# A perceiver kernel: the running maximum of the first attention in float32r, turned by products with the identity

## The chip, the cores and the metric

The kernel runs on one core of a Trainium2 chip. The metric is the device time of one execution in microseconds; for a set of runs the median is given. A core has five engines that run side by side, each strictly in the order of its own queue: TensorE (PE; its weight loads are shown apart as PEld), VectorE (DVE), ScalarE (ACT), GpSimd (POOL) and SyncE (SP), which in this kernel issues the transfers. Products are written to PSUM; all else lies in SBUF or in the chip's main memory.

## The reference

Eight batches of 64 tokens of width 512 (`x`) pass six residual blocks. The first is a cross attention with a context of 1601 rows for each batch: 32 query heads share 8 key and value heads of width 128. The kernel's part at issue is its softmax.

```
q = (query @ Wq + bq).reshape(B, L, NKV, G, HDIM)        # 8 key heads, 4 query heads each
k_, v_ = jnp.split(kv @ Wkv + bkv, 2, axis=-1)
scores = jnp.einsum('blkgd,bmkd->bkglm', q, k) * scale
attn = jax.nn.softmax(scores, axis=-1)
o = jnp.einsum('bkglm,bmkd->blkgd', attn, v).reshape(B, L, NHEAD * HDIM)
return o @ Wo + bo
```

Then follow a state-space block (a scan over the tokens), a linear layer with ternary weights, a second cross attention on the raw context, a causal self attention and a gated feed-forward block, each on the layer-normed result of the one before.

## The kernel before

**Units.** The first attention is worked through in 64 units, one for each batch and key head. A unit handles 256 query columns (4 heads of 64 tokens) against 13 tiles of 128 context rows (the last has 65). Most of its products are float32r products of split operands: a number is kept as a high part in float32r and the rest, and three products (high-high, high-low, low-high) replace one in float32. `x_v` (L338) makes the values, `x_k` (L367) the keys, `x_s` (L389) the scores, `x_av` (L472) the weighted sum, `x_o` (L482) the softmax's denominator and `x_wo` (L522) the output product for pairs of batches. Values, keys, scores and the output product rotate through four PSUM buffers with the tag `kv`.

**The maximum.** Scores lie with the context rows on the partitions. While `x_s` makes them, two tiles at a time, ScalarE copies them from PSUM to the tile `S` (L392) and VectorE keeps an elementwise running maximum in `mx`, 128x512 (L396; L394 for the last tile of 65 rows; L399 folds the two halves to 128x256). In the next unit, `x_max` turns the two 128x128 halves of `mx` over on TensorE into the PSUM tile `m_ps` (L407), so that VectorE can take the maximum along the free axis (L409, to the float32r column `mc`, negated). `x_spread` spreads that column over all partitions by two float32r products, the column broadcast as the stationary operand and the identity as the moving one (L416). `x_exp` adds the result to the scores on VectorE (L430), takes the exponential on ScalarE (L431) and sums on GpSimd. The subtracted value is the same for all rows of a query column and cancels in the quotient.

**Order.** The rest of the blocks run as "side" generators between the steps of the attention, for groups of two batches: `halves` and `prep` lay out split and ternary weights in memory, and `chain` runs blocks two to six for a group. `run` advances them by costs that are written in the file. The program so recorded goes through a scheduler that moves instructions by its own estimate of their times, within their dependences; side instructions are partly pinned to program order. When the attention's last unit is recorded, the pools of the attention are freed, and the fourth group's chain runs with larger pools beside what is left of the third group's. In that last stretch the third group takes weights into `w_r` (L768) and multiplies by L777 and L778; the fourth group's self attention is the lines L1183 to L1226 with its output product at L761, and its feed-forward block begins at L1271. L1284 ends a SiLU with the gate's product, L1294 transposes its result, and L1306 is the last addition.

Of the kernel before, what the change touches and what calls it, by code (L numbers as in the profile page):

```python
# [8 lines left out]
FP = mybir.dt.float32  # L9
FR = mybir.dt.float32r  # L10
AF = mybir.ActivationFunctionType
ALU = mybir.AluOpType
# [4 lines left out]
P = 128  # L17
# [33 lines left out]
def rows_of(t):  # L51
    return TAIL if t == 12 else P
# [26 lines left out]
class Kernel:  # L79
# [293 lines left out]
    def x_s(self, b, i, st):  # L373

        nc = self.nc
        q = self.q[(b, i)]
        S = self.S.setdefault((b, i), [])
        if st == 0:
            self.mf[(b, i)] = self.sb("mx", [P, 2, 256], pool=self.xp, bufs=1)
        mx = self.mf[(b, i)]  # L380
        for g in [(2 * st, 2 * st + 1)] + ([(12,)] if st == 5 else []):
            sp = self.px.tile([P, 2, 256], FP, name=self.nm("s_ps"), tag="kv", bufs=KVB)
            r = P
            for gi, t in enumerate(g):
                r = rows_of(t)
                blk, o = self.at(t)
                kt = self.kt[(b, i, blk)]
                for k, (a, m) in enumerate(((0, 0), (0, 1), (1, 0))):
                    nc.tensor.matmul(sp[:r, gi, :], lhsT=kt[:, a, o : o + r], rhs=q[:, m, :], start=k == 0, stop=k == 2)  # L389
            s = self.sb("S", [P, 2, 256], pool=self.xp, bufs=SB)  # L390
            n = len(g)
            nc.scalar.copy(s[:r, :n], sp[:r, :n])  # L392
            if n == 1:
                nc.vector.tensor_tensor(mx[:r, 0], sp[:r, 0], mx[:r, 0], ALU.max)  # L394
            elif len(S) > 0:
                nc.vector.tensor_tensor(mx, sp, S[0] if len(S) == 1 else mx, ALU.max)  # L396
            S.append(s)
        if st == 5:
            nc.vector.tensor_tensor(mx[:, 0], mx[:, 0], mx[:, 1], ALU.max)  # L399

    def x_max(self, b, i):

        nc = self.nc
        m = self.mf.pop((b, i))
        ps = self.px.tile([P, 2, 256], FP, name=self.nm("m_ps"), tag="m", bufs=MB)
        for h in range(2):
            nc.tensor.transpose(ps[:, 0, h * P : (h + 1) * P], m[:, 0, h * P : (h + 1) * P], self.ident)  # L407
        col = self.sb("mc", [P, 2], FR, pool=self.xp, bufs=2)
        nc.vector.tensor_reduce(col, ps[:, 0].rearrange("p (h k) -> p h k", k=P), AX.X, ALU.max, negate=True)  # L409
        self.mm[(b, i)] = (ps, col)  # L410
# [1107 lines left out]
```

## Time and profile before

| What | Value |
|---|---|
| Median of 3 runs | 2667.18 us (2663.71 to 2670.01) |
| The profiled execution | 2656.56 us, its span 2654.8 us |
| PE, PEld busy | 2513.8 us (95%), 2241.6 us (84%) |
| DVE, ACT, POOL busy | 1671.4 us (63%), 1366.8 us (51%), 1291.8 us (49%) |
| Granted TensorE clock | 0.984 of full speed |
| The transposes L407, the spreading L416 | 128 instructions each |
| The running maximum L396, L394, L399 | 320, 64 and 64 instructions; 218.6, 26.8 and 36.5 us on DVE |

The span is what the profiler saw from the first to the last instruction; the execution's time includes what lies around it. A line of a group names the source line, the engine, the operation, the tile written and the tiles read, then how many there were. In lists of instructions in order of time the first column is the start in the span, the second the length, and a bracket at the end tells how long the engine had been idle and what ended that. Products of TensorE overlap, so their lengths add up to more than the time that passes; the distance from one start to the next tells what an instruction costs.

### The profile page before, as it was taken

What the parts mean: (1) busy time and instruction counts of PE and PEld (TensorE: products, weight loads), DVE (VectorE), ACT (ScalarE), POOL (GpSimd) and SP (SyncE); (2) the same over time, 40 slices, a digit from 0 to 9 for tenths busy, and PEclk for the clock granted to TensorE, in tenths of its full rate; (3) what the DMA queues carried; (4) which work ended last, traced back from release to release, by engine and by line L of the source; (5) the groups of instructions that cost most, each with busy time, mean ns of one, the idle gap of its engine ahead of it and who ended that gap; (6) DMA issues with size and microseconds to landing.
All of it is one profiled execution on the core that took longest, in us unless ns stands there. A gap on an engine that the chain in (4) does not pass through costs nothing. (4 is left out here: it accounts for less than half of the span.)

```text
span 2654.8 us, 43902 instructions
## 1 busy us (share of the span) xinstructions
PE 2513.8 (95%) x16192; PEld 2241.6 (84%) x16192; DVE 1671.4 (63%) x2747; ACT 1366.8 (51%) x3205; POOL 1291.8 (49%) x1305
## 2 busy tenths in 40 slices
PE   7999999999999999999999989999999999876888
PEld 6999899989989999987989888997898988864545
DVE  4545457665687766544567777554557687668755
ACT  4555554444556555544455555544456555445534
POOL 2445563463378655421356667632138467605420
PEclk9999999999999999999999999999999999987899
DMA  9799776675213244765425533654533543367676
GB/s 300 231 311 301 249 262 202 209 240 168 78 50 108 83 130 138 221 196 152 151 61 163 172 114 97 235 166 146 166 121 107 159 152 122 122 216 240 201 253 227
DMA packets 307672, 466.08 MB, mean 176 GB/s; under 512 B 91129, under 2 KB 187385, under 8 KB 302977
## 3 DMA queue, kind: packets, MB, share of 16 engines
q1 hardware_dynamic: 307456, 463.28, 54.2%
q8 instruction: 127, 2.08, 0.3%
q14 instruction: 89, 0.72, 0.1%
HBM read 389.66 MB, written 73.53 MB: 174 GB/s over the span
## 5 line engine op out<-in xcount | busy, mean ns | idle before, releaser
L367 PE MATMUL k_ps<-cxb,wk 128*128 128x384 f32 x2304 | 463.2, 343 | 28.3 <-ACT cxb L105 10.3
L338 PE MATMUL v_ps<-wv,cxb 128*128 128x256 f32 x3456 | 463.9, 282 | 1.3 <-DVE kt L109 1.2
L338 PEld LDWEIGHTS v_ps<-wv,cxb 128*128 128x128 f32 x3456 | 436.6, 189 | 16.7 <-issue 9.1
L367 PEld LDWEIGHTS k_ps<-cxb,wk 128*128 128x128 f32 x2304 | 399.2, 190 | 48.1 <-ACT cxb L105 10.7
L389 PE MATMUL s_ps<-q,kt 128*128 128x256 f32 (+1 forms) x2496 | 410.9, 298 | 9.6 <-DVE mx L396 4.2
L472 PE MATMUL o_ps<-S,v 128*128 128x256 f32 (+1 forms) x1664 | 409.9, 379 | 0.7 <-ACT v L341 0.4
L389 PEld LDWEIGHTS s_ps<-q,kt 128*128 128x128 f32 (+1 forms) x2496 | 338.9, 185 | 31.2 <-DVE mx L396 5.2
L460 POOL TENSOR_TENSOR ss<-ss,S 128x512 f32<-128x512 f32 x254 | 351.4, 1383 | 13.9 <-ACT S L431 0.9
L392 ACT COPY S<-s_ps 128x512 f32<-128x512 f32 (+1 forms) x448 | 241.8, 553 | 219.7 <-PE s_ps L389 216.2
L396 DVE TENSOR_TENSOR mx<-s_ps,mx 128x512 f32<-128x512 f32 x256 | 175.1, 684 | 285.0 <-ACT S L392 284.3
L472 PEld LDWEIGHTS o_ps<-S,v 128*128 128x128 f32 (+1 forms) x1664 | 298.7, 189 | 34.1 <-issue 1.4
L433 POOL TENSOR_TENSOR ss<-S,S 128x512 f32<-128x512 f32 x64 | 83.7, 1308 | 424.7 <-ACT S L431 377.0
L430 DVE TENSOR_TENSOR S<-S,m_ps 128x512 f32<-128x512 f32 (+1 forms) x448 | 257.8, 640 | 19.6 <-PE m_ps L416 19.4
L431 ACT ACTIVATE S<-S 128x512 f32<-128x512 f32 (+1 forms) x448 | 247.0, 600 | 44.3 <-DVE S L430 44.1
L108 ACT ACTIVATE kt<-k_ps,c_bk 128x384 fp32r<-128x384 f32 (+1 forms) x256 | 151.8, 593 | 211.9 <-PE k_ps L367 211.3
L109 DVE SCALAR_TENSOR_TENSOR kt<-k_ps,c_bk,kt 128x384 fp32r<-128x384 f32 (+1 forms) x256 | 160.7, 628 | 132.3 <-ACT kt L108 131.7
L341 ACT COPY v<-v_ps 128x256 f32<-128x256 f32 (+1 forms) x416 | 151.7, 368 | 162.2 <-PE v_ps L338 157.9
L338 PE MATMUL v_ps<-wv,cxt 128*128 128x256 f32 (+1 forms) x1536 | 208.6, 285 | 3.4 <-DVE kt L109 2.5
L338 PEld LDWEIGHTS v_ps<-wv,cxt 128*128 128x128 f32 (+1 forms) x1536 | 194.2, 177 | 12.9 <-DVE kt L109 3.8
L65 DVE TENSOR_TENSOR_SCAN a<-a,a 128x512 f32<-128x512 f32 x96 | 153.8, 1603 | 66.2 <-POOL a L65 66.0
L367 PE MATMUL k_ps<-cxt,wk 128*128 128x450 f32 x768 | 177.6, 374 | 0.3 <-ACT v L341 0.3
L65 ACT ACTIVATE a<-lv,c_A_log 128x128 f32<-128x128 f32 x384 | 123.2, 393 | 101.6 <-DVE a L65 100.8
(382 smaller groups left out, 3969.9 us busy)
## 6 DMA issues: line engine op xcount, KB each, us to landing
wo<-d_wo SPq DMA_DIRECT2D x127, 512.0 KB, 5.5
wk<-d_wk SPq DMA_DIRECT2D x63, 512.0 KB, 3.8
wv<-d_wv SPq DMA_DIRECT2D x31, 1024.0 KB, 5.8
cst<-in_ctxT_dram SPq DMA_DIRECT2D x96, 192.0 KB, 2.9
d_q<-q_t SPq DMA_DIRECT2D x32, 512.0 KB, 5.1
q<-d_q SPq DMA_DIRECT2D x64, 256.0 KB, 2.8
d_wo<-wo SPq DMA_DIRECT2D x32, 512.0 KB, 5.0
w<-d_wat SPq DMA_DIRECT2D x64, 256.0 KB, 3.3
```

The costliest lines, as they stand in the source:

```text
L65: return lambda *a, **k: self.tc.keep_in_program_order(f(*a, **k))
L108: nc.scalar.activation(hi, src, AF.Identity, bias=bias)
L109: eng.scalar_tensor_tensor(lo, src, bias, hi.bitcast(FP), ALU.add, ALU.subtract)
L338: nc.tensor.matmul(ps[:r], lhsT=cx[:, a, c, o : o + r], rhs=w[:, m, c, :], start=k == 0, stop=k == 11)
L367: nc.tensor.matmul(ps[:, :wd], lhsT=w[:, a, c, :], rhs=cx[:, m, c, :], start=k == 0, stop=k == 11)
L389: nc.tensor.matmul(sp[:r, gi, :], lhsT=kt[:, a, o : o + r], rhs=q[:, m, :], start=k == 0, stop=k == 2)
L392: nc.scalar.copy(s[:r, :n], sp[:r, :n])
L396: nc.vector.tensor_tensor(mx, sp, S[0] if len(S) == 1 else mx, ALU.max)
L430: nc.vector.tensor_tensor(sv, sv, ps[:r, 1:2].to_broadcast([r, w, 256]), ALU.add)
L431: nc.scalar.activation(sv, sv, AF.Exp, scale=ISC)
L460: nc.gpsimd.tensor_tensor(ss, ss, S[n], ALU.add)
L472: nc.tensor.matmul(ps[:, 0], lhsT=self.v[(b, j, t)][:r, hc : hc + P], rhs=S[t // 2][:r, t % 2], start=t == 0, stop=t == NT - 1)
```

## The change

The tile `mx` is declared float32r in place of float32. Every maximum writes it as float32r and reads it back through a float32 view, `mf`. The two transposes of `x_max` become two ordinary products: the half of `mx` is the stationary operand and the float32r identity the moving one. Their number, the tiles and the sizes stay.

```diff
         if st == 0:
-            self.mf[(b, i)] = self.sb("mx", [P, 2, 256], pool=self.xp, bufs=1)
+            self.mf[(b, i)] = self.sb("mx", [P, 2, 256], FR, pool=self.xp, bufs=1)
         mx = self.mf[(b, i)]
+        mf = mx.bitcast(FP)
...
             if n == 1:
-                nc.vector.tensor_tensor(mx[:r, 0], sp[:r, 0], mx[:r, 0], ALU.max)
+                nc.vector.tensor_tensor(mx[:r, 0], sp[:r, 0], mf[:r, 0], ALU.max)
             elif len(S) > 0:
-                nc.vector.tensor_tensor(mx, sp, S[0] if len(S) == 1 else mx, ALU.max)
+                nc.vector.tensor_tensor(mx, sp, S[0] if len(S) == 1 else mf, ALU.max)
             S.append(s)
         if st == 5:
-            nc.vector.tensor_tensor(mx[:, 0], mx[:, 0], mx[:, 1], ALU.max)
+            nc.vector.tensor_tensor(mx[:, 0], mf[:, 0], mf[:, 1], ALU.max)
...
         for h in range(2):
-            nc.tensor.transpose(ps[:, 0, h * P : (h + 1) * P], m[:, 0, h * P : (h + 1) * P], self.ident)
+            nc.tensor.matmul(ps[:, 0, h * P : (h + 1) * P], lhsT=m[:, 0, h * P : (h + 1) * P], rhs=self.ident_r, start=True, stop=True)
```

## The prediction

> **What bounds the kernel now.** I read the page's totals first, then the slices, then the table of stretches.
>
> ```profile
> span 2654.8 us, 43902 instructions
> PE 2513.8 (95%) x16192; PEld 2241.6 (84%) x16192; DVE 1671.4 (63%) x2747; ACT 1366.8 (51%) x3205; POOL 1291.8 (49%) x1305
> PE   7999999999999999999999989999999999876888
> ```
> ```profile
> 100.00:700.00 600.00, 590.62 (x3846) 556.07 (x3844) 346.70 (x606) 306.08 (x643) 297.59 (x278) 1.00 0.72 235
> 1300.00:1900.00 600.00, 582.42 (x3819) 521.69 (x3818) 380.99 (x599) 310.93 (x748) 311.63 (x316) 0.99 0.46 145
> 2330.00:2655.00 325.00, 252.16 (x1449) 166.76 (x1447) 214.24 (x418) 151.85 (x407) 94.94 (x100) 0.91 0.69 232
> ```
>
> In the stretches the columns after the length are the busy time of PE, PEld, DVE, ACT and POOL. Up to 2330 us TensorE is all but full: what it must issue sets the time, and every nanosecond of its issue counts. In the last 325 us it is busy for 252, so some 73 us are waits; there the order of its queue decides, since its products start in that order.
>
> The lines that the change touches are these, in the view of the tile `m_ps` (minimum, median, maximum in ns):
>
> ```profile
> L407 PEld LDWEIGHTS m_ps<-ident,mx x128: 137/140/144, 82.3 to 2332.9; 128*128 128x128 f32 x128
> L407 PE MATMUL m_ps<-ident,mx x128: 270/272/329, 82.4 to 2333.0; 128*128 128x128 f32 x128
> L416 PEld LDWEIGHTS m_ps<-ident,mc x128: 185/188/330, 86.0 to 2336.3; 128*128 128x128 f32 x128
> L416 PE MATMUL m_ps<-ident,mc x128: 219/273/415, 86.1 to 2336.4; 128*128 128x128 f32 x128
> ```
>
> L416 is the row to price by: it is already a pair of float32r products of a 128x128 operand with the identity, into the same PSUM tile. Durations overlap, so the cost is read from starts, in the timeline of PE:
>
> ```profile
> 82.43 0.38 PE L407 MATMUL m_ps<-ident,mx 128*128 128x128 f32 x2
> 82.56 0.96 PE L389 MATMUL s_ps<-q,kt 128*128 128x256 f32 x6
> ...
> 86.15 0.34 PE L416 MATMUL m_ps<-ident,mc 128*128 128x128 f32 x2
> 86.32 0.92 PE L338 MATMUL v_ps<-wv,cxb 128*128 128x256 f32 x6
> ```
>
> The work after a pair of transposes starts 0.13 us after the pair, the work after a float32r pair 0.17 us after it. Over all pairs the medians are 139 ns (61 pairs) and 170 ns (62 pairs), counted from when the pair could start to the next start. Inside, the two differ: the second transpose starts 108 ns after the first and the next product 28 ns later; the second float32r product starts 60 ns after the first and the next 110 ns later, because the weight load of the following product is what is late (loads start 108 ns apart).
>
> **The change, part by part.**
>
> *TensorE.* 64 heads times one pair: 64 x (170 - 139) ns = **+2.0 us**, all of it on the bound engine. Bounds: if the products ran 60 ns apart with nothing late behind, 120 ns a pair, -1.2 us; if each kept the 111 ns of the steady 128-column products of L962, 222 ns, +5.3 us. I take 170, from the same form.
>
> [...]
>
> *VectorE.* 448 instructions now write float32r (320 of L396, 64 each of L394 and L399). The rows of one operation in both types, PSUM and SBUF in, 512 wide: 681 ns to float32 (x19) and 683 ns to float32r (x11). 448 x 2 ns = 0.9 us on an engine at 63%: **0**. TensorE's long work beside it hides it; uncovered it would cost those 0.9 us.
>
> *Latency.* From the first start to the end of the second transpose it is 108 + 271 = 379 ns, of a float32r pair 60 + 273 = 333 ns: the reduction L409 may start 46 ns sooner. TensorE waits for it (L416 on L409) 5 times, 4.1 us in all up to 2330 us: at most 5 x 46 ns = 0.2 us, taken as 0. Nothing new is queued behind a wait: instructions, tiles and dependences are the same in number on all five engines.
>
> *Order.* The scheduler, which places instructions by its own estimates, builds another order. In the two built programs the first 575 of 14,400 TensorE instructions stand alike; 3785 stand elsewhere, 228 by over 30 places, 2291 of them in the last quarter. On SP 285 of 1307 moved (231 in the last quarter, 17 places at most), on POOL 259 of 1310 (at most 13). Up to 2330 us I take **0** for this: moved products are neighbours whose inputs mostly are ready, and TensorE's waits there are only 47 us, of many causes.
>
> In the last stretch two groups of batches run side by side: the third's products are L777/L778 on `w_r`, the fourth's the runs L1217, L1224, L761 and then L1271. Timeline of PE, before:
>
> ```profile
> 2606.58 0.43 PE L1224 MATMUL acc<-b,b 128*32 128x64 f32 x16
> ...
> 2613.43 0.60 PE L1294 MATMUL acc<-ident,b 128*128 128x128 f32 x4
> ...
> 2632.23 0.60 PE L1294 MATMUL acc<-ident,b 128*128 128x128 f32 x4
> 2634.49 0.50 PE L777 MATMUL acc<-w_r,b_r 128*128 128x512 f32 x1 [1.66 <-ACT b_r L105]
> ```
> ```profile
> 2622.10 10.02 PEld L1271 LDWEIGHTS acc<-s,b 128*128 128x128 f32 x48
> 2622.34 10.06 PE L1271 MATMUL acc<-s,b 128*128 128x512 f32 x48
> ```
> ```profile
> 2627.75 0.69 DVE L1284 TENSOR_TENSOR b<-b,b 128x512 f32<-128x512 f32 x1
> ```
>
> The fourth group's L1271 ran from 2622.34, and the third's second L1294 (with 16 products after it) only behind them. After the change these stand ahead of L1271, and so L1271 must wait for the third group's SiLU, which L1284 ended at 2628.44. The third group's first L1294 (2613.43 before) also moves forward, ahead of three rounds of L1224 that ran from 2606.58, which is 6.85 us earlier if its inputs allow. I take 6 of these: L1284 ends at 2622.4, plus transposes 0.6, copy and split 0.8, eight 512-wide products at 0.23 and eight 336-wide at 0.155 (3.1), makes L1271 start at about 2627.0: **+4.7 us**. If the third group is no earlier (its weights `w_r<-d_gu` came late then, 0.29 us of wait at 2605.24 with a transfer just landed), it is 2628.44 + 4.5 = 2632.9, about +10; if it is early enough, 0, or a gain of 3.4 us from work that no longer lies at the end.
>
> At the end of the attention the change gains: the last head's L416 ran at 2336.31, behind products that waited for a weight transfer, and now stands behind one float32 product of 0.8 us, at about 2333.9, 2.4 us sooner. It reaches the end only if the fourth group is what is late; with L1271 waiting for the third, it is swallowed. Taken as **0**, bound -2.4.
>
> Sum: 2.0 + 4.7 = **+6.7 us**. The profiled execution took 2656.56 us (span 2654.8 plus 1.8 around it), which would become 2663.3. It lies 10.6 us under the median of the three runs, 2667.18; on that scale the change gives **2674 us**. About 0.2% (5.3 us) is what a measurement can tell from no change; the three runs themselves spread over 6.3 us.
>
> **The rivals.**
>
> *Only the products' price counts* (same). The moves cancel: +2.0, or -0.4 with the earlier end of attention; 2667 to 2669. For it: nothing in dependences or work changes, and TensorE is 98% busy before 2330 us. Against it: the last stretch is all waits, and its order is much changed.
>
> *The waits for attention's PSUM buffers shrink* (faster). These rows are TensorE waiting until VectorE or ScalarE has emptied one of the four `kv` buffers:
>
> ```profile
> PE k_ps L367 <- DVE mx L396: 7.7, 6, 2.3
> PE s_ps L389 <- DVE mx L396: 4.2, 4, 1.9
> PE k_ps L367 <- DVE kt L109: 3.8, 3, 1.6
> PE v_ps L338 <- DVE kt L109: 3.7, 5, 1.1
> ```
>
> With L389 on L109, L367 on L394 and the small ones they make 26.8 us, and products of `o_ps`, which need no such buffer, change places with those that do. A third going is 8.9: 2.0 - 8.9 = -6.9, 2660 us. It decides once over 7.3 us (5.3 + 2.0) of the 26.8 go. Against it: waits can as well be made as lost.
>
> *The product is dearer than L416* (slower): 222 ns a pair, +5.3 us, 2672.5 with no loss by order. For it: L416's weights are one broadcast column, here they are a full matrix. Against it: both loads last 188 ns.
>
> That the change does nothing is excluded: another instruction form is issued.
>
> **How the numbers follow.** Forecast 0.38, dearer product 0.08, only the price 0.30, shrunken waits 0.24: slower 0.46, same 0.30, faster 0.24. The forecast's own range runs from L1271 at +0 (2.0) to L1271 at +10 with the product at its dearest (15.3): 2669 to 2682. For 8 in 10 the half spread of the three runs, 3.2, is added at the far ends: -6.9 - 3.2 gives 2657, 15.3 + 3.2 gives 2685.
>
> **What would show it.** Right: the pair of the new line to the next start near 0.17 us; its weight loads at 188 ns; L396 at 684 ns; TensorE's busy time up by some 2 us; L1271 starting behind a wait for the third group's products, 5 us later counted from the end of attention. Wrong: L1271 without a wait ahead of it and the last stretch shorter; the waits on `mx` and `kt` clearly away from 26.8 us; or a pair at over 0.2 us.

## The result: 0.8% slower, and the profile after

The changed kernel takes 2682.97 us (median; 2681.13 to 2685.43), the kernel before, on the same chip, 2665.44 us (2661.32 to 2670.01). The ratio is 1.0080, 95% interval 1.0063 to 1.0098: some 17 to 26 us slower. Slower was forecast, but as 2674 us. Lines behind L381 have moved on by one: L408 is the old L407, L1272 the old L1271.

The page's totals, and TensorE's slices:

```profile
span 2683.6 us, 43899 instructions
PE 2528.5 (94%) x16192; PEld 2253.8 (84%) x16192; DVE 1679.7 (63%) x2747; ACT 1364.1 (51%) x3205; POOL 1287.0 (48%) x1305
PE   7999999999999999999999989999999998966887
```

The span is 28.8 us longer than that of the profiled execution before (2656.56 us, quicker than the four above, while the one here is the slowest of its four, so the medians differ by less), and TensorE is busy for 14.7 us more. Up to 2330 us it is busy for 2261.6 and 2261.7 us: the difference comes to light at the end. The table of stretches of the changed kernel, for what comes behind 2330 us (the column behind GpSimd's is the granted clock, as a share of full speed):

```profile
2330.00:2690.00 360.00, 266.83 (x1471) 181.44 (x1470) 219.96 (x423) 155.21 (x417) 93.89 (x101) 0.86 0.63 211
```

The same stretch before had 252.16 us of TensorE (1449 records) at a granted clock of 0.91; here it is 266.83 us at 0.86. Part of that "busy" time goes with waiting: in e13 below, products of 512 columns behind a wait of 6.07 us run at a granted clock of 0.50 and last 0.63 us in place of 0.39. In the traces of the two kernels TensorE waits for over 4 us ten times behind the first 10 us (four times before, six in the changed kernel), and the granted clock of the 2 us behind each of these waits is 0.50.

The edited instructions, by the tile `m_ps` (durations as minimum/median/maximum in ns), and from the page's groups:

```profile
L408 PEld LDWEIGHTS m_ps<-ident,mx x128: 186/188/333, 80.1 to 2333.0; 128*128 128x128 f32 x128
L408 PE MATMUL m_ps<-ident,mx x128: 219/273/474, 80.2 to 2333.1; 128*128 128x128 f32 x128
L417 PE MATMUL m_ps<-ident,mc x128: 219/273/454, 83.9 to 2335.2; 128*128 128x128 f32 x128
```
```profile
L397 DVE TENSOR_TENSOR mx<-s_ps,mx 128x512 fp32r<-128x512 f32 x256 | 175.2, 684 | 286.7 <-ACT S L393 286.0
```

L408 has become L417's twin, as priced: counted from start to next start, the new pair takes 171 ns (median of 60 pairs; forecast 170), and the last one starts at 2333 us in both kernels. What the edit does directly is as forecast, and it is not the loss. The waits of TensorE show new rows:

```profile
PE acc L1295 <- DVE b L1285: 9.1, 2, 5.4
PE acc L778 <- ACT a L65: 6.1, 1, 6.1
PE acc L1218 <- POOL b L1210: 4.7, 1, 4.7
```

The first is the wait that was forecast: L1272 stands behind the third group's transposes L1295, and these wait for its SiLU, L1285. The timeline of PE there:

```profile
2644.70 1.09 PE L1295 MATMUL acc<-ident,b 128*128 128x128 f32 x4 [5.44 <-DVE b L1285]
2645.58 1.06 PE L731 MATMUL acc<-ident,b 128*128 128x128 f32 x4
...
2651.00 10.09 PE L1272 MATMUL acc<-s,b 128*128 128x512 f32 x48
```

L1272 starts 28.7 us later than before, and the end comes 28.8 us later.

### The profile page after: what moved, and what is told of

The parts are those of the page before. It is cut to its first block, busy times and chain, and to the rows that moved or that the text cites. A ratio compares the mean times of both kernels' runs of the same rounds, so it can differ in the third digit from the quotient of the medians.

```text
span 2683.6 us, 43899 instructions
## 1 busy us (share of the span) xinstructions
PE 2528.5 (94%) x16192; PEld 2253.8 (84%) x16192; DVE 1679.7 (63%) x2747; ACT 1364.1 (51%) x3205; POOL 1287.0 (48%) x1305
## 4 chain that ended last, share of the span: by engine, by line
PE 62%; DVE 12%; POOL 9%; DMA 7%; ACT 5%; issue 4%; SPq 0%; POOLq 0%; DVEq 0%; ACTq 0%
PE v_ps L338 14%; PE k_ps L367 14%; PE o_ps L473 8%; PE s_ps L390 7%; POOL a L65 4%; DVE a L65 4%; POOL ss L461 3%; PE acc L278 3%; PE w_ps L523 2%; PE acc L823 2%; PE acc L1048 2%; PE acc L778 2%; PE acc L1105 1%; PE acc L779 1%; ACT S L432 1%
## 5 line engine op out<-in xcount | busy, mean ns | idle before, releaser
L367 PE MATMUL k_ps<-cxb,wk 128*128 128x384 f32 x2304 | 463.0, 344 | 31.0 <-ACT cxb L105 10.2
L338 PE MATMUL v_ps<-wv,cxb 128*128 128x256 f32 x3456 | 463.1, 281 | 1.6 <-DVE kt L109 1.5
L338 PEld LDWEIGHTS v_ps<-wv,cxb 128*128 128x128 f32 x3456 | 436.7, 189 | 14.1 <-issue 6.7
L367 PEld LDWEIGHTS k_ps<-cxb,wk 128*128 128x128 f32 x2304 | 401.0, 191 | 50.4 <-DVE mx L397 11.0
L397 DVE TENSOR_TENSOR mx<-s_ps,mx 128x512 fp32r<-128x512 f32 x256 | 175.2, 684 | 286.7 <-ACT S L393 286.0
L338 PE MATMUL v_ps<-wv,cxt 128*128 128x256 f32 (+1 forms) x1536 | 206.8, 283 | 2.7 <-DVE kt L109 1.7
L338 PEld LDWEIGHTS v_ps<-wv,cxt 128*128 128x128 f32 (+1 forms) x1536 | 192.6, 175 | 11.4 <-DVE kt L109 2.8
L367 PE MATMUL k_ps<-cxt,wk 128*128 128x450 f32 x768 | 179.0, 376 | 0.0
## 6 DMA issues: line engine op xcount, KB each, us to landing
q<-d_q SPq DMA_DIRECT2D x64, 256.0 KB, 2.8
w<-d_wat SPq DMA_DIRECT2D x64, 256.0 KB, 3.1
```

Source lines behind the costliest of these rows:

```text
L338: nc.tensor.matmul(ps[:r], lhsT=cx[:, a, c, o : o + r], rhs=w[:, m, c, :], start=k == 0, stop=k == 11)
L367: nc.tensor.matmul(ps[:, :wd], lhsT=w[:, a, c, :], rhs=cx[:, m, c, :], start=k == 0, stop=k == 11)
L397: nc.vector.tensor_tensor(mx, sp, S[0] if len(S) == 1 else mf, ALU.max)
```

## The experiments

The first question was whether the product or the order makes the loss. For that a kernel is given a written order: the list `ORDER` holds each engine's queue of a built program, and each instruction gets an edge to the one ahead of it. The edges order the issue and make no engine wait for another; e1 and e2 show that they cost nothing that can be measured (e1 takes 2.3 us more than the kernel before, the product's price among them; e2 takes 2683.01 us, the changed kernel in the same order 2682.97). (In the file the list is packed.)

```diff
+def as_written(tc):
+    here = {i.name: i for i in tc.nc.cur_bb.bb.instructions}
+    info = mybir.DependencyInfo(mybir.DependencyClass.NoSync, mybir.DependencyReason.DATA)
+    for ids in ORDER.values():
+        for last, n in zip(ids, ids[1:]):
+            tc.add_manual_dep(here[f"I-{n}"], f"I-{last}", info, reason="order")
...
     Kernel(ctx, tc, ins, out).run()
+    as_written(tc)
```

"Old order" is the order of the kernel before, "new order" that of the changed kernel; a time, such as 2300 us, is that of an instruction's start in the kernel before. All differences in us are against the median of the kernel before on the same chip in the same series (2660.8 for e1 to e4, or 2659.9 without one execution of 8947 us, 2657.7 for e5 to e8, 2658.9 for e9 to e12, 2661.4 for e13 to e16).

### The product, the order and the type, each alone

**e1**: the changed kernel with every queue in the old order.

> The changed kernel (float32r maximum, float32r products), with every engine's queue held in the order that the kernel before had, by edges between neighbours in a queue that order their issue and add no wait. Theory A (the queues' order makes the loss, the product itself costs its issue time): the pair of L408 stays at 170 ns to the next start, and the time is 2 us over the kernel before, 1 to 5 us over at most (ratio about 1.001). Rival B (the product or the float32r maximum itself makes the loss): the time stays near the changed kernel's, some 17 us over before (ratio about 1.006 or more).

Measured: 2663.07 us, ratio 1.0007 (0.9991 to 1.0023): +2.3 us, no difference that can be told from none.

**e2**: the kernel before, with its transposes, in the new order.

> The other half of the same question: the kernel before, float32 transposes and float32 maximum, with every queue held in the order of the changed kernel. Theory A: 2 us under the changed kernel, so some 15 us over before (ratio about 1.006), with the last stretch beginning some 12 us later than in the kernel before. Rival B: within 0.2% of before.

Measured: 2683.01 us, ratio 1.0084 (1.0058 to 1.0109): +22.2 us.

**e3**: the new type of `mx`, with the transposes kept; its order is the old one by itself.

```diff
-            nc.tensor.transpose(ps[:, 0, h * P : (h + 1) * P], m[:, 0, h * P : (h + 1) * P], self.ident)
+            nc.tensor.transpose(ps[:, 0, h * P : (h + 1) * P], m[:, 0, h * P : (h + 1) * P].bitcast(FP), self.ident)
```

> The float32r maximum alone: mx is declared and written in float32r, and turned over by the same float32 transposes through a float32 view. The built queues are those of the kernel before. Theory A: the same time as before within 0.2%, L397 at 684 ns as before. Rival B, if the type of the maximum is what costs: slower by a good part of the 17 us.

Measured: 2658.38 us, ratio 0.9992 (0.9976 to 1.0008).

The order alone makes the whole loss, as far as the intervals tell, and neither the product nor the type makes a measurable part of it. What is left is where in the order it lies.

### Where in the order

**e4** was to hold the new order up to 2300 us and the old one behind. The two lists had been exchanged in writing it, so what ran is its mirror: the old order up to 2300 us, the new one behind. Its expectation reads the other way round.

> The changed kernel with float32r products; the queues stand in the changed order for everything that the kernel before had started by 2300 us of its span, and in the order of the kernel before for all the rest (the end of attention and the last stretch). If the loss is made in the last stretch (theory A1: the third group's last loads and products stand behind attention's there): at most 5 us over before. If it is made by the changed order before 2300 us, where side work lies 7 us later at 1600 to 2200 us (A2): 10 us or more over before, as the lag is carried into the last stretch.

Measured: 2679.38 us, ratio 1.0070 (1.0045 to 1.0096): +18.6 us. Read as what it is: the order behind 2300 us is enough for most of the loss.

**e5 to e8** are true to their labels; each is the changed kernel with a list joined from the two.

```diff
-ORDER = the old order
+ORDER = e5: new up to 2300, old behind | e6: old up to 2385, new behind
+        e7: new up to 2385, old behind | e8: new, but old from 2300 to 2385
```

> The changed kernel with every queue in the changed order for what had started by 2300 us and in the old order for the rest. (The run labelled e4 was the mirror of this and of its own label: its list was written from exchanged orders, so it held the old order up to 2300 us and the changed order behind, and its 2679.4 us speak for the last stretch.) On the scale of that day's old kernel, 2661 us. Theory A1, the order of the last stretch makes the loss: 2663 to 2668, the 2 us of the product and what the third group lags at 2300. Theory A2, the order before 2300 makes it: 2679 or more. Parts of both: between.

Measured: 2672.42 us, ratio 1.0055 (1.0038 to 1.0072): +14.7 us.

> The changed kernel, old order up to 2385 us (the end of the third group's state-space block and the start of the fourth group's chain), changed order behind. Theory T1, the loss is the third group's state-space tail, 12 us late at 2366, and all later delay is its consequence: 2663 to 2666. Theory T2, the order of what follows makes its own loss (the wait of L1272 for the third group's L1285, forecast at 4.7 us): 2668 for the forecast's size, up to 2679 if it makes the whole growth from 12 to 29 us.

Measured: 2674.43 us, ratio 1.0058 (1.0039 to 1.0078): +16.7 us.

> The changed kernel, changed order up to 2385 us, old order behind. Theory T1: 2675 (12 us late and no more) to 2690 (the delay grows whatever the order behind). Theory T2: 2663 to 2668 if the old order behind 2385 takes the delay back, 2675 if the two add up, 12 us from the tail and the rest from behind.

Measured: 2670.19 us, ratio 1.0050 (1.0030 to 1.0071): +12.5 us.

> The changed kernel in its own order, but with the old order between 2300 and 2385 us, where the third group's gate projections L823 and their transfers from in_W_inT_dram stand before the attention's last products and not behind them. Theory T1: the third group's last residual comes some 8 to 12 us sooner and the time is 2663 to 2671. Theory T2: 2677 to 2683, the order behind 2385 makes its loss all the same.

Measured: 2681.60 us, ratio 1.0085 (1.0068 to 1.0103): +23.9 us.

Neither A1 nor A2, and neither T1 nor T2, holds alone: the order up to 2300 us and the order behind 2385 us each make a loss, and e8 shows that mending what lies between them saves nothing.

A table of stages, from the traces of the profiled executions, sorts this. o and n are old and new order up to 2300, from 2300 to 2385, and behind. "At 1900" is how much later than before the instructions between 1900 and 2000 us start (median). "Residual" is the third group's last addition of the state-space block, behind which the fourth group's layer norm stands on VectorE in every run; it is given as it was, and less what the run was late at 1900.

| Run | Order | At 1900 | Attention's last product | Residual | less "at 1900" | Residual to L1271/L1272 | From there to the end |
|---|---|---|---|---|---|---|---|
| before | o o o | 0 | 2355.9 | 2367.4 | 2367.4 | 255.0 | 32.4 |
| e1 | o o o | -3.2 | 2353.4 | 2365.9 | 2369.1 | 255.1 | 33.7 |
| e3 | o o o | -0.4 | 2351.9 | 2364.8 | 2365.2 | 258.4 | 32.4 |
| e6 | o o n | 2.6 | 2355.6 | 2367.8 | 2365.2 | 272.9 | 32.4 |
| e4 | o n n | 4.2 | 2350.7 | 2377.9 | 2373.7 | 271.5 | 32.0 |
| e5 | n o o | 8.7 | 2370.3 | 2383.0 | 2374.3 | 258.8 | 32.8 |
| e7 | n n o | -3.6 | 2343.4 | 2369.7 | 2373.3 | 264.3 | 34.0 |
| e8 | n o n | 0.1 | 2360.8 | 2373.2 | 2373.1 | 272.9 | 32.4 |
| e2 | n n n | 4.7 | 2352.2 | 2378.3 | 2373.6 | 272.7 | 32.4 |
| changed | n n n | 7.4 | 2354.6 | 2379.4 | 2372.0 | 271.6 | 32.6 |

What the runs are late by at 1900 us scatters over 12 us among those with the same order (-3.6 to 8.7 with the new one). With the old order it scatters over 9 us (-5.2 in e15 below, 4.2 in e4). It is left out of what follows; that the new order itself costs a few us up to 1900 us can't be told from these single profiles, nor excluded. Two stages then carry the loss. The residual comes some 6 us later in the runs whose order is new up to 2300 us, and in e4 (2372.0 to 2374.3 against 2365.2 to 2369.1); e16 below, with the order of e4 up to 2385 us, has 2370.5, so 3 us of such a difference can be chance. And from the residual to L1272 the new order behind 2385 takes 271.5 to 272.9 us, where the old one takes 255.0 to 264.3 (255.0, 255.1 and 258.4 where it is old throughout). The last column changes by 2 us at most. Some 6 and 17 us make 23, in the interval of 17 to 26.

### The first stage: the third group is late at the attention's end

With the new order up to 2300 us, the third group's work between 2250 and 2300 us lags 13 us behind the attention's (changed kernel: median of 71 instructions +17.4 us against the kernel before, the attention's own 352 +4.8; in e2, e5, e7 and e8 the lag is 11 to 12). The lag grows from 2000 us on. On GpSimd the attention's sums stand ahead of the side work; the changed kernel's timeline of POOL:

```profile
2052.23 1.31 POOL L434 TENSOR_TENSOR ss<-S,S 128x512 f32<-128x512 f32 x1 [2.65 <-ACT S L432]
2053.61 5.82 POOL L461 TENSOR_TENSOR ss<-ss,S 128x512 f32<-128x512 f32 x4
2059.40 1.22 POOL L65 TENSOR_TENSOR b<-b,a1m 128x512 f32<-128x512 f32 x1
```

and before, where the same product of `b` and `a1m` was ahead of them:

```profile
2042.04 1.05 POOL L65 TENSOR_TENSOR b<-b,a1m 128x512 f32<-128x512 f32 x1
...
2045.35 1.30 POOL L433 TENSOR_TENSOR ss<-S,S 128x512 f32<-128x512 f32 x1
```

(It comes 17.4 us later, the attention's sum ahead of it 6.9. The swap is one step of the lag, not its start: the side work's product of `b` and `c_hmask` ahead of it is already 12.5 us late, at 2042.40 after 2029.92. No step of the lag was tried alone.) The lag is then paid in one of two ways. If the old order follows (e5), the attention waits for it: on VectorE its maximum L410 stands behind the third group's scan, and on TensorE L417 waits for L410. DVE and PE of e5:

```profile
2317.23 2.31 DVE L65 TENSOR_TENSOR_SCAN a<-a,a 128x512 f32<-128x512 f32 x1 [1.83 <-POOL a L65]
2319.47 0.39 DVE L410 TENSOR_REDUCE mc<-m_ps 128x2 fp32r<-128x256 f32 x1
```
```profile
2319.91 0.69 PE L417 MATMUL m_ps<-ident,mc 128*128 128x128 f32 x2 [11.53 <-DVE mc L410]
```

If the new order follows, the attention goes ahead, and four of the eight rounds of the third group's gate projections L823 are left behind its last product (a round is four products in the program and eight records in the trace). PE of the changed kernel:

```profile
2328.95 1.16 PE L823 MATMUL acc<-a,a 128*128 128x128 f32 x8 [1.01 <-DMA a<-in_W_inT_dram]
...
2354.17 0.86 PE L523 MATMUL w_ps<-wk,ot 128*128 128x512 f32 x3
...
2360.16 1.13 PE L823 MATMUL acc<-a,a 128*128 128x128 f32 x8 [2.58 <-DMA a<-in_W_inT_dram]
...
2370.41 0.79 PE L778 MATMUL acc<-lv,a 128*128 128x512 f32 x1 [6.09 <-ACT a L65]
```

In e1, with the old order, four of these rounds are done by 2321 us, while TensorE has the attention's products beside them (it is busy for 16.45 of the 20 us from 2300 us on):

```profile
2310.02 1.16 PE L823 MATMUL acc<-a,a 128*128 128x128 f32 x8 [2.11 <-DMA a<-in_W_inT_dram]
2316.69 1.95 PE L823 MATMUL acc<-a,a 128*128 128x128 f32 x16
2320.50 1.05 PE L823 MATMUL acc<-a,a 128*128 128x128 f32 x8
```

Their transfers stand in SP's new order behind others (of `lv`) that hold the queue up for 5.85 us. SP of the changed kernel:

```profile
2349.80 0.37 SPq L820 DMA_DIRECT2D a<-in_W_inT_dram  x1
2350.22 5.85 SPq L772 DMA_DIRECT2D lv<-d_wout  x2
2356.16 1.77 SPq L820 DMA_DIRECT2D a<-in_W_inT_dram  x3
```

**e16** takes the second way alone, without the lag: the new order from 2300 to 2385 us, the old one ahead and behind.

> The changed kernel, changed order between 2300 and 2385 us alone, old order ahead and behind: 16 gate projections of the third group stand behind the attention's last product. If they hold up the third group's last residual and with it the whole chain of the fourth group: 25 us in place of 12 from the attention's last product to the residual, 2672 to 2675. If the old order behind takes the delay back: 2661 to 2666.

Measured: 2666.56 us, ratio 1.0020 (1.0007 to 1.0034): +5.2 us. The residual does come 27.0 us behind the attention's last product, but this product comes at 2343.8 us (the run stood at +0.3 us at 1900), 12.1 us sooner than before, since the gate projections no longer stand in its way. The residual, at 2370.8, is 3.5 us late. So of the 15.5 us by which the group's tail is longer, 12 are given back, and the window by itself is worth 3 us beside the product's 2. The time lies just above the second expected value, 2661 to 2666 us, and well below the first.

### The second stage: whose products stand ahead

**e13** does the forecast's own step alone, without the head start that the forecast gave the third group. On TensorE, ScalarE and VectorE, what the third group starts between 2622 and 2638 us is put ahead of what the fourth group starts there; the rest is the old order.

```diff
-ORDER = the old order
+ORDER = the old order, but from 2622.3 to 2638.25 us on PE, ACT and DVE: third group first, then fourth
```

> The changed kernel in the old order, but for the step that was forecast: on TensorE, ScalarE and VectorE the third group's transposes L1295 and the 16 products behind them stand ahead of the fourth group's L1272 and what follows from it, as in the changed order. The old order with the product would be about 2661 us. Forecast: L1272 starts 4.7 us later, 2666, with its bounds 2661 and 2671. If this step is the whole loss behind 2385 us: 2677.

Measured: 2674.52 us, ratio 1.0051 (1.0034 to 1.0068): +13.1 us. That is beyond the forecast's upper bound of 2671. For a third group that comes no sooner the forecast had about 10 us, and 2 for the product. PE before and of e13:

```profile
2619.25 0.60 PE L730 MATMUL acc<-ident,b 128*128 128x128 f32 x4
...
2622.34 10.06 PE L1271 MATMUL acc<-s,b 128*128 128x512 f32 x48
```
```profile
2624.10 0.60 PE L731 MATMUL acc<-ident,b 128*128 128x128 f32 x4
...
2633.35 1.09 PE L1295 MATMUL acc<-ident,b 128*128 128x128 f32 x4 [6.07 <-DVE b L1285]
2635.11 0.79 PE L778 MATMUL acc<-w_r,b_r 128*128 128x512 f32 x1 [0.68 <-ACT b_r L105]
...
2636.86 0.63 PE L779 MATMUL acc<-w_r,b_r 128*128 128x512 f32 x1
...
2640.24 10.09 PE L1272 MATMUL acc<-s,b 128*128 128x512 f32 x48
```

From L731 to L1272 it takes 16.1 us; before, from L730 at 2619.25 to L1271 at 2622.34, it took 3.1. Of the difference of 13.0 us, 6.07 are the wait for L1285. The rest, 6.9 us, is the third group's work, for which the forecast had 4.5. Most of the excess is in the eight 512-wide products: from the first start to the end of their turn they take 3.9 us (the last six follow one another at 0.43 us), where the forecast had eight times 0.23. The granted clock in e13's table of stretches goes with it:

```profile
2627.00:2633.00 6.00, 0.28 (x2) 0.00 (x0) 2.99 (x5) 2.46 (x4) 0.00 (x0) 0.93 0.56 204
2633.00:2639.00 6.00, 4.97 (x13) 3.49 (x14) 0.90 (x2) 0.58 (x1) 0.00 (x0) 0.50 0.01 3
2639.00:2650.00 11.00, 11.00 (x56) 9.54 (x55) 0.43 (x1) 3.17 (x6) 0.00 (x0) 1.00 0.51 165
```

After the wait of 6.07 us, TensorE's granted clock is 0.50 for some 5.6 us, counted from the transposes L1295, or 3.9 us from the first product behind them, and then 1.00 again. In the changed kernel, behind its wait of 5.44 us for L1285, the products of 512 columns last 0.59 to 0.79 us up to 2649.06 us and 0.40 us from there on: 4.4 us from the transposes, 2.6 us from the first product on `w_r` behind them. What sets the length of these stretches no run here shows.

In the changed kernel the step lies in the same place, but costs less there, where the fourth group is already late when it comes to it: from its last self-attention residual to L1272 it takes 11.7 us, against 8.7 before. The other 14 us of the stage come ahead of that. In e6 the fourth group's state-space block takes 146.3 us from the residual of the first stage in place of 139.9 (up to 143.4 in other runs with the old order there), and its self attention ends 114.2 us behind that block in place of 106.3 (up to 110.1), with this wait on the way:

```profile
2573.58 1.12 PE L1218 MATMUL acc<-ident,b 128*128 128x128 f32 x4 [4.66 <-POOL b L1210]
```

while the third group's self attention starts ahead of the old order (the second round of its transposes L1160, L1161 there, starts at 2527.9 us in e6, at 2543.9 before) and still ends no sooner (its residual comes at 2583.6 us in e6, at 2584.0 before). Counted in the built programs, 30 of the third group's products on `w_r` stand behind the first L1271 in the old order and 14 behind L1272 in the new one: 16 have gone ahead of it.

**e14 and e15** part the second stage by time.

```diff
-ORDER = the old order
+ORDER = e14: old up to 2560, new behind | e15: old, but new from 2385 to 2560
```

> The changed kernel, old order up to 2560 us, changed order behind. Between the third group's end of the state-space block and L1272 the old order takes 255 us and the changed one 272, of which 6 before the fourth group's own state-space block ends and 11 behind it. If the 11 us are made by the order of the self attention and the feed-forward block: 2670 to 2674. If they follow from what the order between 2385 and 2560 us set up: 2661 to 2664.

Measured: 2685.74 us, ratio 1.0092 (1.0066 to 1.0117): +24.4 us, above both expected values; 281.5 us from the residual to L1272, of which the fourth group's self attention takes 127.6 (106.3 before).

> The changed kernel, changed order between 2385 and 2560 us alone, old order ahead and behind. If the fourth group's state-space block is what this order delays: its last residual L988 comes 6 us later and the time is 2666 to 2669. If its effect is given back: 2661.

Measured: 2661.77 us, ratio 1.0000 (0.9982 to 1.0017): +0.4 us; 257.0 us from the residual to L1272. In e15 what the fourth group's state-space block loses (144.9 us) is given back in the self attention (102.7); the order behind 2560 us is what costs. It costs more still when it doesn't follow the order that it was built for. A likely reason, not tried alone: in e14 the third group has not run ahead by 2560 us (the second round of L1161 starts at 2547.0 us, in e6 at 2527.9), and its products stand ahead of the fourth group's all the same.

### Can the loss be read off by counting?

By then the case looked as if two counts carried it: gate projections behind the attention's last product (old 0, new 16) and products on `w_r` behind the first L1271 (old 30, new 14). **e9 to e12** are four builds whose order comes from the scheduler itself, with other combinations of the two.

```diff
 e9, on the changed kernel, in advance():
-                        c["got"] += next(c["gen"])
+                        if c["env"]["tail"]:
+                            with self.tc.high_priority(40):
+                                c["got"] += next(c["gen"])
+                        else:
+                            c["got"] += next(c["gen"])
 e10, on the changed kernel:
-            nc.tensor.matmul(ps[:, 0, h * P : (h + 1) * P], lhsT=m[:, 0, h * P : (h + 1) * P], rhs=self.ident_r, start=True, stop=True)
+            nc.tensor.transpose(ps[:, 0, h * P : (h + 1) * P].bitcast(FR), m[:, 0, h * P : (h + 1) * P], self.ident_r)
 e11, on the kernel before, and e12, on the changed one:
-SPAN = [2.6,2.6,2.6,0.2]
+SPAN = [2.6,2.6,2.65,0.2]
```

> The changed kernel, the fourth group's instructions given precedence of 40 places over the others in the scheduler; its order then differs from the changed one only behind 2390 us. Counted in the built program, 16 gate products of the third group stand behind the attention's last product (old kernel 0, changed 16), and 30 of the third group's products on w_r stand behind the fourth group's first L1272 (old 30, changed 14). Theory C, that these two counts carry the loss, some 12 us for the first and 16 us for the second: L1272 no longer waits for the third group's L1285, and the time is that of e7, 2668 to 2674. Theory R, that any new order scatters by itself without these counts saying which: no more than chance would have it within 2655 to 2690.

> The changed kernel with its two products written as transposes of the float32r tile, which come with a third order of their own: 0 gate products behind the attention's last product as in the old kernel, 14 products on w_r behind the first L1272 as in the changed one. Theory C: the price of the second count alone, as e6, 2672 to 2679, with the third group's L1285 ahead of L1272. Were it the product itself that costs, 2658 to 2663.

> The old kernel, the third group's chain spread over 2.65 in place of 2.6 batches of the attention: 0 gate products behind the attention's last product, 38 products on w_r behind the first L1271 (old 30). Theory C: no loss, 2652 to 2663, and faster than the old kernel unless the third group's own end becomes the last. Theory R: as above.

> The changed kernel with the same 2.65: 12 gate products behind the attention's last product, 38 products on w_r behind the first L1272. Theory C: the price of the first count alone, 2666 to 2674. Theory R: as above.

| Run | Measured, us | Ratio (95%) | Attention's last product to the residual | Residual to L1271/L1272 | From there to the end |
|---|---|---|---|---|---|
| e9 | 2694.04 | 1.0136 (1.0116 to 1.0156) | 26.6 | 282.2 | 38.9 |
| e10 | 2688.25 | 1.0109 (1.0091 to 1.0127) | 10.0 | 286.9 | 31.9 |
| e11 | 2673.49 | 1.0046 (1.0029 to 1.0063) | 11.2 | 256.0 | 43.9 |
| e12 | 2687.10 | 1.0098 (1.0079 to 1.0118) | 21.3 | 258.6 | 44.0 |

All four are slower than theory C had them, and it falls as a price. Theory R, that new orders scatter by themselves, had 2655 to 2690 us; three of the four lie in it, and nothing here decides it. The first count tells the length of the tail (not its price, as e16 shows): 10 to 11 us without gate projections behind the attention, 21 to 27 us with 12 or 16 of them (11.5 to 12.9 in the runs above where the order from 2300 to 2385 us is old, 24.7 to 27.2 where it is new). The second doesn't: e9 has the old count and takes 282 us all the same. And where 38 products are left behind L1271, the stage is short (256 and 259 us), but the third group is now itself late, and the last column grows by 11 us; in e11 TensorE then waits 10.6 us for L1284. In these builds, then, leaving more of either group behind the other did not pay. The float32r transposes of e10 are the cheapest of the three forms, with a median of 123 ns from the pair's start to the next start (137 for the old transposes read the same way, 171 for the products), and e10 is the second slowest of the six orders: the order outweighs the instruction. Of the six orders that came from the scheduler itself (those of before, of the changed kernel and of e9 to e12), the old one is the fastest by 14 us or more. No build was measurably faster than the kernel before.

## Why the prediction was wrong, point by point

- **What bounds the kernel: right, but not enough.** Up to 2330 us TensorE is full in both kernels (busy for 2261.6 and 2261.7 us), and the last transposes start at 2332.8 us in both; the difference of the two profiled executions comes to light in the last 350 us. But of the gate projections' eight rounds four were done by then before, and one in the changed kernel.
- **TensorE's pair, +2.0 us: right.** 171 ns a pair, and e1 measures +2.3 us (from -2.4 to +6.1) for the whole edit in the old order; the interval fits the 2.0 and does not prove it. The load of 188 ns has come; the dearer product of 222 ns has not, and with it that rival falls. The 171 ns are 32 ns a pair more than the 139 of the transposes, too little to be seen in the time.
- **VectorE and latency, 0: right.** L397 lasts 684 ns, as L396 did before, and e3 measures no loss for the type (ratio 0.9992).
- **"Up to 2330 us I take 0 for this": this step failed.** The argument was that moved products are neighbours whose inputs are ready, and it looked at TensorE's waits alone. TensorE hardly waits more there (its waits from 100 to 2330 us add up to 51.6 us before, not 47, and to 52.6 after). But the third group's side work falls 13 us behind the attention on the other queues, without any trace of it in TensorE's busy time, and it is paid at the attention's end, with some 6 us up to the residual; e5, with the new order up to 2300 us and the old one behind, takes 14.7 us more, the product's 2 among them. The full engine showed that nothing was lost yet; it did not show that nothing was owed.
- **The last stretch, +4.7 us: the mechanism was right, the term too small.** This is the second step that failed (its own terms add up to 4.6). L1272 does stand behind a wait for L1285, for the reason given, and the step alone, with no head start, costs 13.1 us with the product (e13), some 11 without; the whole stage grows by 17. Counted from the attention's last product, L1272 starts 296.4 us later, before 266.4: 30 us more, where the forecast had 5. What was wrong in its working is "I take 6 of these": the third group's SiLU was taken to come 6 us sooner because its transposes move forward in the queue. In the changed kernel these transposes do stand ahead of the rounds (of L1225 there), and still start at 2627.09 us, 13.7 us after the 2613.43 of before; those behind the SiLU start at 2644.70, 12.5 us after the 2632.23 of before. (12.0 us of each were owed at the residual already; the rest is 1.7 and 0.5 us later, not 6 sooner.) Moving forward was relative: the third group went ahead of the fourth, and neither got earlier. What its products then cost the fourth group ahead of L1272 was not charged at all, though the rounds that they overtake were named; it is 14 of the stage's 18 us in e6. And the eight products behind the wait were charged at 1.8 us and took 3.3, in e13 3.9.
- **End of the attention, gain taken as 0: right in size, wrong in what happens there.** The last L417 does start sooner, at 2334.97 us in place of 2336.31, and it is indeed swallowed. Not by L1272's wait, but by the third group's gate projections, which the products of the attention have overtaken.
- **Rivals.** "Only the products' price" is what e1 and e3 measure, and what the change would have cost with its order kept. "The waits for the `kv` buffers shrink" is not to be seen: the waits of L338, L367 and the scores on `mx` and `kt` up to 2330 us add up to 26.3 us after 24.9.

The time of 2683 us lies inside the range, at its upper end, and beyond the forecast's own range of 2669 to 2682. That it lies inside is in part luck: the upper end holds 3.3 us for a dearer product that did not come, and the loss up to the attention's end is not in it. What the joined orders are worth doesn't add up: e5 and e6 make 14.7 and 16.7 us, together 29 with the product counted once, where both at once made 17 to 26. A loss made by the seam between two orders could be one reason: in e7 the old order behind the new one takes 264.3 us, against 255.0 to 258.4 where it is old throughout. But e5's 258.8 hardly lies outside that, so where the rest of e5's loss is made stays open.

## What to carry to other kernels

When a scheduler builds the order, an edit that costs 2 us can come with an order that costs 20, in places that have nothing to do with the edit: pin the old order and measure the edit in it before judging the edit. Compare the two built orders engine by engine, and ask of each group's work that goes ahead whose work it delays; a full TensorE can hide side work that is falling behind on GpSimd, VectorE and ScalarE (13 us here) until the moment when it is waited for. A count of what stands ahead shows where to look, but it did not price the orders here.

## What the hardware showed that was not expected

In e13 a wait cost more than its length: TensorE's clock was granted at 0.50 for some 5.6 us behind a wait of 6.07 us, and a product of 512 columns lasted 0.63 us there against 0.39 elsewhere. Over everything behind 2300 us the granted clock was 0.92 before and 0.88 in the changed kernel, while it was 0.99 and 1.00 ahead of it: in this stretch of waits, the later order also had the lower clock.

Executions with equal order scatter over 12 us in how far they are at 1900 us, where TensorE is full (busy for 485.1 of the 500 us from 1800 us on before, for 486.7 in the changed kernel), while the stage from the residual to L1272 repeats within 1.4 us in the five runs that share its order (271.5 to 272.9 us). The old order doesn't repeat as well (255.0, 255.1 and 258.4 us in before, e1 and e3), so a difference of 3 us in that stage can't be read from one profile; 16 us can.
